# Cross-attention in fp32: one bias sum moved from VectorE to ScalarE and accumulating transfers, and two small reorderings of VectorE's queue

## The chip, the cores and the metric

The kernel runs on one core of one Trainium2 chip. The metric is the device time of one execution in microseconds (us). It is compared as the median of several runs.

## The reference

Two cross-attention layers, one after the other, on 8 batches of 100 queries (width 1024) and 1444 context rows (width 512), all in fp32:

```python
def _L0_xattn_ref(query, key, Wq, bq, Wk, bk, Wv, bv, Wo, bo):
    Q = query @ Wq + bq
    K = key @ Wk + bk
    V = key @ Wv + bv
    weights = softmax(Q @ K.T * scale, axis=-1)        # over the context
    return query + (weights @ V) @ Wo + bo

def _L1_xattn_ref(emb, latent, Wq, bq, Wk, bk, Wv, bv, gamma, beta):
    q, k, v = emb @ Wq + bq, latent @ Wk + bk, latent @ Wv + bv
    w = softmax(q @ k.T * scale, axis=1)               # over the queries
    x = w @ v + emb
    return (x - mean(x)) * rsqrt(var(x) + EPS) * gamma + beta
```

## The kernel before

The kernel never forms K or V. It multiplies weights with weights first: `qk0` = Wq Wk^T of layer 0, `vo0` = Wv Wo of layer 0, later `qk1` for layer 1. Queries then meet the raw context (`s` tiles), the softmax weights are transposed, and the weighted context rows (`A`) go through `vo` (layer 0, the projection, tiles `o_...`) or through Wv (layer 1). Bias terms become sums: the bias that bv brings to the output is bv times Wo, a sum over the 1024 rows of Wo, each scaled by one entry of bv.

The large products use a scheme of seven products of halves in place of eight (the left matrix in blocks A11 to A22, the right in B11 to B22). It needs sums of blocks, S1 to S4 on the left and T1 to T4 on the right, which VectorE makes. Several partial results share banks of PSUM (the matmul accumulators): X, Z, Y and W are such banks. `put` copies a finished bank to SBUF, by ScalarE; `add` adds one to what is already there, by VectorE. A product that accumulates further into a bank has to wait until the `put` or `add` before it has read that bank. An inner call of the same scheme (`inner_product`) splits one of the seven once more; its banks are named `vo_w_x`, `vo_w_z`, `o_w_x` and so on.

TensorE's order is written out by hand (`manual_schedule`). VectorE's calls go through a helper on line 96, so most of its rows have that line; where `vector.in_order` is true they stay in the written order. Each engine works through its own queue in order, so an instruction that waits holds all that stands behind it.

The first place of the change is `weight_products` for `vo0`. The matrices come in eight `unit` tiles (called `vo` in the trace), each with one row block of Wv^T and one of Wo; rows 0 to 3 are blocks 11 and 12 of both sides, rows 4 to 7 blocks 21 and 22. TensorE runs X (A11 B11), Z (A12 B21), Y (S1 T1), then X again with S2 T2. VectorE makes S1 and T1, then T3 (in place of B12), S3 (in place of A21), T2 (in place of B11), later S2 (in place of S1) and T4 (in place of B21). The tiles that hold S1 and then S2 are `vo_s`.

The bias sum of `vo0` is started by `accumulate(1)`, line 465, which calls `transferred_sum` (line 543). Its first half scales rows 0 to 3 of Wo on ScalarE into four tiles (`scaled_sum`, line 569) and adds the tiles pairwise by accumulating transfers issued by GpSimd (`transfer_added`, line 566). Its second half, `second_half`, scales and adds rows 4 to 7 on VectorE in one tile (`prob` in the trace) and adds that by one more transfer. `accs[scaled[0][0]][1]()` calls this second half, on line 500. The finished sum is transposed on VectorE much later (line 585, at 125.35 us).

The second place is `project0` for layer 0, lines 1076 to 1090. There two products in halves run side by side: the outer one uses the banks X_ and Y, an inner one, the generator `W`, yields after each of its seven products. `next(W)` runs the first of them.

Of the kernel before, what the change touches and what calls it, by code (L numbers as in the profile page):

```python
# [27 lines left out]
ALU = mybir.AluOpType  # L28
# [6 lines left out]
EC, LC = E // P, L // P  # L35
# [20 lines left out]
def two_layer_cross_attention(ctx: ExitStack, tc: tile.TileContext, a: dict, out: bass.AP):  # L56
# [11 lines left out]
    def bank(name):  # L68
        return psum.tile([P, 512], F32, tag="ps", name=name)
# [4 lines left out]
    def unit(name):  # L74
        return stream.tile([P, E + L], F32, tag="unit", name=name)
# [4 lines left out]
    def row(name):  # L80
        return work.tile([P, E], F32, tag="row", name=name, bufs=3)

    def weight_rows(name):
        return work.tile([P, MC * T + QD * (-(-T // QD)) - T], F32, tag="wT", name=name, bufs=3)

    def wide_sums(name):
        return work.tile([P, LC, GT], F32, tag="gT", name=name, bufs=3).rearrange("p c t -> p (c t)")
# [13 lines left out]
    vector = Vector()  # L101
# [38 lines left out]
    def run(*parts):  # L140

        parts = list(parts)
        while parts:
            parts = [g for g in parts if next(g, parts) is not parts]
# [8 lines left out]
    def half_product(banks, lhs, rhs, fresh, nb, width):  # L153

        run(half_steps(banks, lhs, rhs, fresh, nb, width))
# [24 lines left out]
    def combine(to, x, y, op, engine=vector):  # L180
        for t, p, q in zip(to, x, y):
            engine.tensor_tensor(t, p, q, op)

    def chunks(t, n):

        return [t[:, i, :] for i in range(n)]
# [68 lines left out]
    def inner_product(name, lhs, rhs, nb, width, t, put, add, right=None, left=None, ahead=False, spare=bank2):  # L255
# [13 lines left out]
        def room(x, t):  # L269
            t = t.rearrange("p (i n) -> p i n", i=m)  # L270
            return [t] if len(x) == 1 else [t[:, i, :] for i in range(m)]
# [5 lines left out]

        S2, S3, S4, T2, T3, T4 = A11, A21, A12, B11, B12, B21
        if ahead:

            S2, S4 = (room(lhs, t[:, o : o + lw]) for o in (lw + rw, 2 * lw + rw))
            if not right:
# [4 lines left out]
        if left:  # L287
            S1, S2, S3, S4 = left

        def second():  # L290
            combine(T2, B22, T1, ALU.subtract)
            combine(S2, S1, A11, ALU.subtract)

        def fourth():
            combine(T4, B21, T2, ALU.subtract)
            combine(S4, A12, S2, ALU.subtract)

# [8 lines left out]
        def product(ps, left, right, fresh):  # L306
            half_product([ps], left, right, fresh, h, w)

        def steps():
# [15 lines left out]
            yield  # L325
            product(X, S2, T2, False)
            put(0, 1, X)
# [19 lines left out]
    def weight_products(name, left, right, l_width, r_width, scaled, between=None):  # L347
# [33 lines left out]
        accs = {}  # L381
# [42 lines left out]
        def pair(n):  # L424
            return [(bank2 if n == "w" else bank)(f"{name}_{n}{j}") for j in range(2)]
# [4 lines left out]
        def block(r, c, j):  # L430

            n = r * nb + j * per
            return dst[:, n : n + per, c * rh : (c + 1) * rh]

        def put(r, c, banks):
            for j in range(2):
                nc.scalar.copy(block(r, c, j), banks[j].rearrange("p (n w) -> p n w", n=per))  # L437

        def add(r, c, banks):
            for j in range(2):  # L440
                to = block(r, c, j)
                vector.tensor_tensor(to, to, banks[j].rearrange("p (n w) -> p n w", n=per), ALU.add)
# [21 lines left out]
        if name == "vo0":  # L464
            accumulate(1)
        put(0, 0, X)
        vector.in_order = name == "vo0"
        combine(T1, B12, B11, ALU.subtract)
        if name == "qk0":
# [3 lines left out]
            Z = pair("z")  # L473
# [6 lines left out]
            W = pair("w")  # L480
# [3 lines left out]
        else:  # L484
            combine(S1, A21, A22, ALU.add)
            Z = pair("z")
# [9 lines left out]
        if name != "qk0":  # L496
            T2, T4 = B11, B21
            combine(T2, B22, T1, ALU.subtract)
            if name == "vo0":
                accs[scaled[0][0]][1]()  # L500
            add(0, 0, Z)
        combine(S1, S1, A11, ALU.subtract)
        S2 = S1
        if name != "vo0":
            combine(A21, A11, A21, ALU.subtract)
        if name != "qk0":
# [7 lines left out]
        t = wide_sums(f"{name}_t")  # L514
# [28 lines left out]
    def transferred_sum(name, srcs, of):  # L543

        n = EC if of == "qk1" else EC // 2
        tiles = [row(f"{name}_{n}") for n in range(2)] + [weight_rows(f"{name}_2")[:, :E]]
        tiles += [t[:, :E] for t in prob]  # L550
        if n == EC:
            tiles += [weight_rows(f"{name}_{n}")[:, :E] for n in range(6, 8)]
        scaled_sum(tiles[:n], srcs[:n])

        def second_half():
            t = tiles[n]
            for i, (src, by) in enumerate(srcs[n:]):
                if i == 0:
                    vector.tensor_scalar(t, src, by, None, ALU.mult)
                else:  # L560
                    vector.scalar_tensor_tensor(t, src, by, t, ALU.mult, ALU.add)
            transfer_added(tiles[0], t)

        return tiles[0], second_half

    def transfer_added(to, t):
        nc.gpsimd.dma_start(out=to, in_=t, accum_op=ALU.add)

    def scaled_sum(tiles, srcs):

        for t, (src, by) in zip(tiles, srcs):
            tc.keep_in_program_order(nc.scalar.activation(t, src, AF.Copy, scale=by))
        k = 1
        while k < len(tiles):
            for i in range(0, len(tiles) - k, 2 * k):
                transfer_added(tiles[i], tiles[i + k])
            k *= 2
# [231 lines left out]
    def first_block_sums():  # L809
# [3 lines left out]
    vo0 = weight_products(  # L813
        "vo0", "L0_xattn_WvT", "L0_xattn_Wo", L, E, (("L0_xattn_bv", 1),), first_block_sums
    )
# [197 lines left out]
    def project0(AS, A0):  # L1013

        B11, B21, B12, B22 = ([A0[g][:, 2 * k + i, :] for i in range(2)] for g in range(2) for k in range(2))
        t12, t4 = (work.tile([P, LC, GT], F32, tag="gT", name=f"o0_t{n}", bufs=3) for n in (12, 4))
        T1, T2, T3, T4 = chunks(t12, 2), [t12[:, 2 + i, :] for i in range(2)], B12, chunks(t4, 2)  # L1020
        h = GT // 2
        room, right = unit("o0_t"), [[t4[:, 2 + n // 2, n % 2 * h : n % 2 * h + h]] for n in range(4)]

        def pair(n, bank=bank):
            return [bank(f"o0_{n}{j}") for j in range(2)]

        def product(banks, lhs, rhs, fresh):
            half_product(banks, lhs, rhs, fresh, 2, GT)

        def add(j, r, g, banks):  # L1030
            e = 4 * j + 2 * r
            add_to_queries([e, e + 1], g * GT, GT, banks)

        def inner(n, j, R, G, lhs, rhs, t, right=None):
            def add(r, c, ps):
                add_to_queries([4 * j + 2 * R + r], G * GT + c * h, h, [ps])

            return inner_product(f"o0_{n}{j}", lhs, rhs, 2, GT, t, add, add, right, ahead=True)

        (A, S), (A_, S_) = AS  # L1040
        X = pair("x")

        def first():
            yield from half_steps(X, A[0], B11, True, 2, GT)
            add(0, 0, 0, X)
            Z = pair("z")
            yield from half_steps(Z, A[1], B21, True, 2, GT)
            add(0, 0, 0, Z)

        yield first()  # L1050
        vector.in_order = True
        yield inner("z", 1, 0, 0, A_[1], B21, room[:, :512], right)
        combine(T1, B12, B11, ALU.subtract)
        X_ = pair("x")
        product(X_, A_[0], B11, True)
        combine(T2, B22, T1, ALU.subtract)
        add(1, 0, 0, X_)
        Y = pair("y")
        product(Y, S[0], T1, True)
        combine(T4, B21, T2, ALU.subtract)  # L1060
        combine(T3, B22, T3, ALU.subtract)
        add(0, 1, 1, Y)
        product(X, S[1], T2, False)
        add(0, 0, 1, X)
        W = pair("w", bank2)
        product(W, A[3], T4, True)
        add(0, 1, 0, W)
        W = inner("w", 1, 1, 0, A_[3], T4, room[:, 512:])
        product(X, S[2], T3, False)
        add(0, 1, 1, X)  # L1070
        add(0, 1, 0, X)
        product(Y, S[3], B22, False)
        add(0, 0, 1, Y)
        yield

        Y = pair("y")
        product(Y, S_[0], T1, True)
        Q = inner("q", 1, 0, 1, S_[3], B22, room[:, :512], right)
        add(1, 1, 1, Y)
        product(X_, S_[1], T2, False)  # L1080

        next(W)
        add(1, 0, 1, X_)
        run(W)
        add(1, 0, 1, Y)
        product(X_, S_[2], T3, False)
        run(islice(Q, 4))
        add(1, 1, 1, X_)
        add(1, 1, 0, X_)
        run(Q)  # L1090
        vector.in_order = False
# [241 lines left out]
    for bs in SETS:  # L1333
        t = wide(f"A1T_{bs[0]}").rearrange("p c t -> p (c t)")[:, : LC * len(bs) * T]
        t = t.rearrange("p (c t) -> p c t", c=LC)
# [39 lines left out]
```

## Time and profile before

| | us |
|---|---|
| runs shown | 634.80, 634.42, 633.78 |
| median | 634.42 |
| profiled execution, its own time | 634.84 |
| its span in the trace | 632.9 |
| TensorE busy | 621.5 |
| VectorE busy | 487.1 |
| ScalarE busy | 163.9 |

The span is the time from the first to the last recorded instruction. PE is TensorE's matmul side and PEld its loading of weights; DVE is VectorE, ACT ScalarE, POOL GpSimd and SP SyncE, and a "q" behind a name is that engine's issuing of transfers. In rows of groups the name before "<-" is what is written and the names behind it are what is read. In a timeline a row begins with start and duration, and the brackets give the idle time just before it and what ended it. An fp32 matmul appears as two records.

### The profile page before, as it was taken

The numbers are of one execution on the slowest core, as the hardware profiler recorded it, in microseconds if no ns is written. First come the engines' busy times: TensorE is split into PE (matmuls) and PEld (weight loads), VectorE is DVE, ScalarE is ACT, GpSimd is POOL, SyncE is SP. The second block draws the span as 40 slices with busy tenths as digits, with TensorE's granted clock in tenths as the row PEclk, the third lists the DMA queues.
The fourth block names the chain that finished last, engine by engine and source line by source line (L and its number), as shares of the span: only waits on it lengthen the run. The fifth ranks groups of instructions, "written<-read, shape, count | busy, mean of one in ns | idle before, by whom it ended". The sixth has DMA issues, their size and how long they took to land.

```text
span 632.9 us, 10570 instructions
## 1 busy us (share of the span) xinstructions
PE 621.5 (98%) x4142; PEld 534.2 (84%) x4142; DVE 487.1 (77%) x995; ACT 163.9 (26%) x380; POOL 102.2 (16%) x133
## 2 busy tenths in 40 slices
PE   9999999999999999999999999999999999999994
PEld 8886467688985999999989666756999999999992
DVE  2987979996885797666758687968777659898886
ACT  1322012324304234423230001113433240325301
POOL 2110101112230000000000001008111220544054
PEclk9999999999999999999999999999999999999998
DMA  8969848335999788988942308255888990599002
GB/s 272 293 136 348 274 140 272 68 81 111 203 315 382 283 311 299 327 307 306 312 155 88 101 0 325 96 194 192 295 305 307 316 324 2 201 330 332 27 22 84
DMA packets 52521, 138.27 MB, mean 218 GB/s; under 512 B 4403, under 2 KB 8755, under 8 KB 52471
## 3 DMA queue, kind: packets, MB, share of 16 engines
q1 hardware_dynamic: 46792, 120.85, 55.1%
q0 software_dynamic: 5280, 16.26, 11.7%
q8 instruction: 33, 0.54, 0.3%
q10 hardware_dynamic: 398, 0.47, 0.2%
q14 instruction: 18, 0.14, 0.1%
HBM read 123.36 MB, written 3.28 MB: 200 GB/s over the span
## 4 chain that ended last, share of the span: by engine, by line
PE 90%; DMA 3%; DVE 3%; issue 1%; POOL 1%; ACT 0%; POOLq 0%; DVEq 0%; SPq 0%
PE s L923 25%; PE A L894 25%; PE qk_x L163 6%; PE o_x L163 5%; PE g_x L163 4%; DMA vo<-in_L_xattn_Wo 3%; PE o_y L163 3%; PE g_y L163 3%; PE vo_x L163 2%; PE qk_y L163 2%; PE qk_z L163 2%; DVE vo L96 1%; PE o_z L163 1%; PE o_w L163 1%; PE qk_w L163 1%
## 5 line engine op out<-in xcount | busy, mean ns | idle before, releaser
L894 PE MATMUL A<-w,c 120*128 120x100 f32 (+1 forms) x1536 | 249.6, 265 | 0.0
L894 PEld LDWEIGHTS A<-w,c 120*128 120x128 f32 (+1 forms) x1536 | 218.0, 190 | 2.8
L96 DVE STREAM_TRANSPOSE w<-prob 32x384 f32<-32x384 f32 (+1 forms) x256 | 143.7, 561 | 27.6 <-ACT prob L962 9.7
L923 PE MATMUL s<-cT,g1T 128*100 128x131 f32 (+2 forms) x592 | 122.8, 296 | 0.0
L923 PE MATMUL s<-cT,g0T 128*100 128x131 f32 (+2 forms) x592 | 122.7, 296 | 0.0
L923 PEld LDWEIGHTS s<-cT,g1T 128*100 128x100 f32 x592 | 78.4, 167 | 8.6 <-issue 0.3
L923 PEld LDWEIGHTS s<-cT,g0T 128*100 128x100 f32 x592 | 78.2, 167 | 8.4 <-PE c L593 0.4
L935 ACT ACTIVATE prob<-s,c 100x393 f32<-100x393 f32 (+2 forms) x64 | 34.5, 560 | 112.7 <-PE s L923 99.5
L1111 ACT ACTIVATE w<-w,negmax 120x100 f32<-120x100 f32 (+1 forms) x96 | 34.8, 364 | 82.7 <-DVE negmax L96 82.7
L955 DVE TENSOR_REDUCE maxima<-prob 100x1 f32<-100x394 f32 (+3 forms) x32 | 16.5, 528 | 23.4 <-ACT prob L935 23.1
L1321 POOL DMA_DIRECT2D wv<-in_L_xattn_Wv x1 | 0.8, 772 | 191.2 <-PE o_x L163 191.2
L163 PE MATMUL qk_x<-qk 128*128 128x256 f32 x128 | 29.7, 380 | 0.0
L1130 POOL TENSOR_TENSOR part<-w 120x500 f32<-120x500 f32 x8 | 10.9, 1368 | 112.9 <-DVE rstd L1205 28.6
L163 PEld LDWEIGHTS qk_x<-qk 128*128 128x128 f32 x128 | 23.3, 190 | 3.0 <-ACT qk L437 0.2
L669 ACT ACTIVATE g1T<-g_x,k 128x400 f32<-128x400 f32 x4 | 2.4, 594 | 69.2 <-PE g_x L163 69.0
L1111 ACT ACTIVATION_READ_ACCUMULATOR w<-w,negmax 120x1 f32 (+1 forms) x96 | 17.9, 187 | 0.0
L1210 POOL TENSOR_TENSOR z<-z,vectors 100x1024 f32<-100x1024 f32 x7 | 16.5, 2356 | 8.2 <-ACT z L1209 8.2
L96 DVE TENSOR_TENSOR xT<-xT,o_x 128x400 f32<-128x400 f32 (+1 forms) x32 | 15.8, 539 | 2.2 <-PE o_x L163 2.0
L1188 PE MATMUL z<-ident,xT 128*100 128x128 f32 x64 | 16.3, 273 | 0.0
L1209 ACT ACTIVATE z<-z,rstd 100x1024 f32<-100x1024 f32 x7 | 8.0, 1149 | 31.9 <-POOL rstd L1206 31.9
L1192 DVE SCALAR_TENSOR_TENSOR z<-vectors,r,z 100x512 f32<-100x512 f32 x16 | 11.8, 740 | 4.8 <-PE z L1188 4.8
L163 PE MATMUL vo_x<-vo 128*128 128x512 f32 x32 | 15.3, 595 | 0.0
(415 smaller groups left out, 987.8 us busy)
## 6 DMA issues: line engine op xcount, KB each, us to landing
cT<-in_ctxT SPq DMA_DIRECT2D x64, 722.0 KB, 6.3
c<-in_ctx SPq DMA_DIRECT2D x48, 768.0 KB, 8.3
c<-in_ctx SPq DMA_DIRECT2D x16, 512.0 KB, 5.9
vo<-in_L_xattn_Wo SPq DMA_DIRECT2D x8, 512.0 KB, 10.1
qk<-in_L_xattn_WqT SPq DMA_DIRECT2D x8, 512.0 KB
qk<-in_L_xattn_WqT SPq DMA_DIRECT2D x15, 256.0 KB, 5.8
c<-in_ctx SPq DMA_DIRECT2D x16, 224.0 KB, 5.9
xT<-in_xT SPq DMA_DIRECT2D x2, 1600.0 KB
```

Of the source, the lines that this page charges most:

```text
L96: ins = getattr(nc.vector, op)(*args, **kw)
L163: nc.tensor.matmul(banks[n // per][:, n % per * width : (n % per + 1) * width], lhs[i][:, n * P : (n + 1) * P], rhs[i], start=(fresh and i ...
L894: nc.tensor.matmul(ps[:, k * T : (k + 1) * T], c[m // CQ][:r, m % CQ, k * P : (k + 1) * P], w[:r, m, :], start=(m == 0 and k == 0), stop=( ...
L923: nc.tensor.matmul(banks[n // per][:T, cuts[n] - o : cuts[n + 1] - o], q[:, k, t0 : t0 + T], cT[k][:, cuts[n] : cuts[n + 1]], start=(k == ...
L935: nc.scalar.activation(p[:, part], ps[:T, : part.stop - part.start], AF.Identity, bias=key_bias[layer][:T, b : b + 1], scale=SCALE,)
L955: nc.vector.tensor_reduce(maxima[:, n : n + 1], p[:, part], AX.X, ALU.max)
L1111: nc.scalar.activation(w[:r, m0 + m, :], w[:r, m0 + m, :], AF.Exp, bias=negmax[:r, m : m + 1], accum_out=total[:r, m : m + 1])
L1130: add(part, w[:MR, 0:5, :], w[:MR, 5:10, :], ALU.add)
L1188: nc.tensor.transpose(ps[:T, e * P : (e + 1) * P], xT[:, 4 * j + e, b * T : (b + 1) * T], ident)
L1192: nc.vector.scalar_tensor_tensor(z[:, half], bv1[j][:T], s["r"], ps[:T, :], ALU.mult, ALU.add)
L1209: nc.scalar.activation(z, z, AF.Copy, scale=rstd)
L1210: nc.gpsimd.tensor_tensor(z, z, beta[:T], ALU.add)
```

## The change

In `vo0` the second half of the bias sum is made like the first: four scaled tiles by ScalarE, added pairwise by transfers. It is called right after the copies of the first X product, and no longer from VectorE's sequence of sums. Two more tiles of the pool "wT" are taken for it. VectorE's four operations for the sum are gone, GpSimd issues three transfers more. Still in `vo0`, the two additions of Z move behind the four operations that make S2. In `project0` the two additions of X_ move behind four additions of the inner product, where they stood behind one.

```diff
@@ weight_products
         put(0, 0, X)
+        if name == "vo0":
+            accs[scaled[0][0]][1]()
         vector.in_order = name == "vo0"
...
             combine(T2, B22, T1, ALU.subtract)
-            if name == "vo0":
-                accs[scaled[0][0]][1]()
-            add(0, 0, Z)
+            if name != "vo0":
+                add(0, 0, Z)
         combine(S1, S1, A11, ALU.subtract)
         S2 = S1
+        if name == "vo0":
+            add(0, 0, Z)
...
@@ transferred_sum
-        if n == EC:
+        if of != "qk0":
             tiles += [weight_rows(f"{name}_{n}")[:, :E] for n in range(6, 8)]
         scaled_sum(tiles[:n], srcs[:n])
 
         def second_half():
             t = tiles[n]
-            for i, (src, by) in enumerate(srcs[n:]):
-                if i == 0:
-                    vector.tensor_scalar(t, src, by, None, ALU.mult)
-                else:
-                    vector.scalar_tensor_tensor(t, src, by, t, ALU.mult, ALU.add)
+            if of != "qk0":
+                scaled_sum(tiles[n:], srcs[n:])
+            else:
+                for i, (src, by) in enumerate(srcs[n:]):
+                    if i == 0:
+                        vector.tensor_scalar(t, src, by, None, ALU.mult)
+                    else:
+                        vector.scalar_tensor_tensor(t, src, by, t, ALU.mult, ALU.add)
             transfer_added(tiles[0], t)
@@ project0
-        next(W)
+        run(islice(W, 4))
         add(1, 0, 1, X_)
         run(W)
```

## The prediction

> **What bounds the kernel now.** I read the page's busy table first, then the waits of TensorE, then the order of time on TensorE and VectorE around each wait. The table says that TensorE works nearly all the time:
>
> ```profile
> PE 621.5 (98%) x4142; PEld 534.2 (84%) x4142; DVE 487.1 (77%) x995; ACT 163.9 (26%) x380; POOL 102.2 (16%) x133
> ```
>
> So only TensorE's idle time can be saved, unless matmuls go, and the change touches none. The view of TensorE's waits lists every one of them:
>
> ```profile
> PE warm L108 <- DVE ones L105: 1.1, 1, 1.1
> PE vo_x L163 <- DVE vo_s L96: 1.0, 1, 1.0
> PE o_w_y L163 <- DVE xT L96: 0.6, 1, 0.6
> PE g_z_x L163 <- DVE g_t L96: 0.4, 1, 0.4
> ```
>
> The second and third stand at the two places that the change edits. The first is the timeline of VectorE and TensorE near 65 to 75 us (start, duration, what, and in brackets the idle time before it):
>
> ```profile
> 65.41 2.49 DVE L96 TENSOR_TENSOR vo<-vo,vo_s 128x512 f32<-128x512 f32 x4
> 67.82 0.74 DVE L96 TENSOR_SCALAR prob<-vo,L_xattn_bv 128x1024 f32<-128x1024 f32 x1
> 68.60 3.92 DVE L96 SCALAR_TENSOR_TENSOR prob<-vo,L_xattn_bv,prob 128x1024 f32<-128x1024 f32 x3
> 72.44 1.28 DVE L96 TENSOR_TENSOR vo<-vo,vo_z 128x512 f32<-128x512 f32 x2
> 73.63 1.43 DVE L96 TENSOR_TENSOR vo_s<-vo_s,vo 128x256 f32<-128x256 f32 x4
> 74.97 2.49 DVE L96 TENSOR_TENSOR vo<-vo,vo 128x512 f32<-128x512 f32 x4
> ```
>
> ```profile
> 59.27 7.03 PE L163 MATMUL vo_z<-vo 128*128 128x512 f32 x16
> 66.13 7.03 PE L163 MATMUL vo_y<-vo_s 128*128 128x512 f32 x16
> 74.20 7.10 PE L163 MATMUL vo_x<-vo,vo_s 128*128 128x512 f32 x16 [1.04 <-DVE vo_s L96]
> 81.14 1.03 PE L163 MATMUL vo_w_x<-vo 128*128 128x256 f32 x4
> ```
>
> VectorE works through T2, the bias sum (four operations) and the additions of Z before S2; S2's first piece ends about 74.05, and TensorE starts X at 74.20. The second place is in the projection of layer 0:
>
> ```profile
> 374.31 0.50 PE L163 MATMUL o_w_w<-o_t,vo 128*128 128x200 f32 x2
> 375.37 0.60 PE L163 MATMUL o_w_y<-o_t,o_t 128*128 128x200 f32 x2 [0.56 <-DVE xT L96]
> 375.81 0.50 PE L163 MATMUL o_w_x<-o_t,vo 128*128 128x200 f32 x2
> 376.15 2.85 PE L163 MATMUL o_x<-A0T,vo 128*128 128x400 f32 x8
> ```
>
> ```profile
> 373.45 0.36 DVE L96 TENSOR_TENSOR xT<-xT,o_w_x 128x200 f32<-128x200 f32 x1 [0.41 <-PE o_w_x L163]
> 373.73 1.05 DVE L96 TENSOR_TENSOR xT<-xT,o_x 128x400 f32<-128x400 f32 x2
> 374.69 0.35 DVE L96 TENSOR_TENSOR xT<-xT,o_w_z 128x200 f32<-128x200 f32 x1
> 374.96 0.35 DVE L96 TENSOR_TENSOR xT<-xT,o_w_y 128x200 f32<-128x200 f32 x1
> ```
>
> The second Y product overwrites a bank that the addition at 374.96 must have read (done 375.31). That addition stands behind the two of X_.
>
> **What the Trainium skill says.** "Perfetto Trace Analysis", section "Tensor Engine Instruction (MATMUL, LD_WEIGHTS)": the end of a matmul is an estimate, its start is recorded. The trace agrees: the 16 of Z end at 66.30, after Y's start at 66.13. I therefore count from start to start. "ScalarE: Activation LUTs", section "What ACT_TABLE_LOAD costs": an ACTIVATE with one pointer operand takes about 280 ns + 0.833 ns per element, an estimate of 1.13 us for 1024; the trace has 1.149, which I use. "DMA: Bandwidth & Descriptors", sections "SWDGE vs HWDGE vs iDMA" and "Issuing engines are not separate DMA queues": only GpSimd issues accumulating transfers, and all queues share the same 16 engines. All such transfers in the trace stand on GpSimd's queue. "SBUF — State Buffer", section "Who interferes with whom": a tensor_tensor with both inputs in SBUF contends with GpSimd's reads, not its writes; no row here shows such contention, so I bound it below.
>
> **Part 1, the bias sum and S2.** Before, rows 4 to 7 of Wo were summed on VectorE: 0.74 + 3.92 = 4.7 us. Now ScalarE scales each row: 4 x 1.149 = 4.6 us, right after the two copies of X (they start 58.61 and 59.47, end 60.06). It needs the rows of Wo; VectorE's own wait for the last row ended at 63.46, so the rows are there by then. ScalarE ends near 64.7 (60.06 + 4.6; from the last row's landing, 63.46 + 1.15 = 64.6). Behind them on ScalarE stand the copies of Y, which before started at 72.34 after 12.29 us of idle time: cost nothing, with over 7 us of cover. The sum moves to three more transfers on GpSimd (prob1 += prob2, vo_6 += vo_7, prob1 += vo_6), ahead of the last one. Transfers of this size landed 5.6 to 9.0 us after issue, median 8.3. GpSimd issues at 63.37 (as before), about 64.3 and 65.2, then near 74 and 83; the sum is whole near 92 instead of 82. Its reader is the VectorE transpose at 125.35: 33 us of cover. GpSimd's next work stands at 108.01. GpSimd's three issues take 0.86 us each; if each held VectorE up wholly, that is 2.6 us before T2 is done, at 70.5, still ahead of X.
>
> S2 writes over S1 in place, so it cannot all move to 67.9: its four pieces wait for Y's four row blocks. Y's 16 matmuls take 66.13 - 59.27 = 6.86 us; its quarters are over about 67.85, 69.56, 71.28 and 72.99. ScalarE's copy of Y's last bank began 73.20, so a release takes about 0.2. S2's pieces (0.42 each) then end near 68.5, 70.2, 71.9 and 73.6. VectorE sits between them, and Z's additions, T4 and the four W sums are queued behind the fourth. Z's additions run 73.5 to 74.8, T4 74.8 to 77.2, the W sums to 79.4; before, the last two ended 77.4 and 79.6. So nothing gets later, though the 4.7 us that VectorE saves become idle time. TensorE needs S2's first piece at 72.99 and its fourth 5.1 us later, and T4 at 79.85: all there. The copies of X that X's accumulation needs were over at 60.06.
>
> Gain: without the stall X starts at 72.99 instead of 74.20, and the next group at 66.13 + 2 x 6.86 = 79.85 instead of 81.14: **1.29 us** (the wait view's 1.04 is the lower reading).
>
> What is late next: VectorE idles 2.16 us before 81.77 and 0.96 before 84.00, each time released by TensorE. With TensorE 1.29 earlier and VectorE 0.2 ahead, about 1.1 of the first is left and the 0.96 stays. VectorE is nearly full from there to 110, but its work starts from these releases and moves with them. So the stall of 0.4 at 108.31 stays, and the loads of the next weights (issued from 84.78 as matrices come free) move too.
>
> **Part 2, the projection.** The additions of w_z, w_y and the second w_x go ahead of X_'s two. From TensorE's starts plus the 0.2 release, VectorE runs them at 373.79, 374.13 and 374.51, and X_'s at 374.79 and 375.27. The addition of w_y ends 374.48, so the second Y product starts 0.34 after w_w, at 374.65; w_x follows at 374.99 (its bank free at 374.92), o_x at 375.33. o_x overwrites X_'s first bank, read until 375.31, with 0.06 to pass on (375.31 to 375.37 above): 375.37. Its second bank is free at 375.85, needed at 376.04. Gain 376.15 - 375.37 = **0.78 us** (lower reading 0.56). VectorE's next wait, 1.43 us for o_q_x, shows it isn't behind; nothing is late next.
>
> Sum: 1.29 + 0.78 = 2.07. The profiled execution's own time is 634.84 with a span of 632.9: span to 630.8, own time to 632.8. The median of the runs shown is 634.42, 0.42 lower; minus 2.07 it is **632.4**.
>
> **The rivals.** *Only part of a stall goes.* If S2's pieces were all held to Y's end (73.2), X would start near 73.7: part 1 brings 0.5, the sum 1.3, 633.1. If X_'s additions keep o_x waiting, part 2 brings nothing: 633.1 too. If both, 633.9. Against: S2 is four operations on separate row blocks; for: margins of 0.04 to 0.1 us in part 2. *The gain is given back* at 108.31, if VectorE does not move with TensorE: the stall grows by 1.29, leaving 0.78, 633.6. Against: the idle 0.96 at 84.00. *Slower: the three transfers hold up xT.* They fall in the stretch where the DMA engines are full:
>
> ```profile
> 60.00:70.00 10.00, 10.00 (x25) 4.38 (x24) 8.70 (x16) 0.05 (x1) 0.85 (x1) 1.00 1.07 333
> 70.00:80.00 10.00, 8.96 (x22) 3.86 (x21) 9.58 (x20) 1.17 (x2) 0.86 (x1) 1.00 0.67 201
> 80.00:90.00 10.00, 10.00 (x36) 6.35 (x35) 7.26 (x23) 2.66 (x6) 0.00 (x0) 1.00 0.32 93
> ```
>
> (the last two columns are the DMA share and GB/s). xT was issued at 53.17, behind the last row of Wo; SyncE issues nothing between 64.37 and 84.78. The share falls to 0.67 in 70 to 80, so I take xT as landed near 77; its first use is the product at 100.2, now 98.9. It decides once xT is over 22 us later. At worst all three, at 9.0 us, go ahead of it: 77 + 27 = 104, TensorE waits 5.1, net +3.0: 637.4. Sharing makes it far less likely.
>
> **Numbers.** Both stalls go 0.70; partly 0.13; given back 0.07; slower 0.10, with what I don't see. A measurement of this kernel tells some 0.2% (1.27 us) from no change: the partial cases lie around that edge. Faster 0.74, same 0.15, slower 0.11. Range 631.5 (the third stall of 0.4 goes too, and the runs' own spread of half a us) to 634.4 (partial cases and given back; it leaves out the slower one).
>
> **What would show it.** TensorE's waits without vo_x and o_w_y; X 6.86 us after Y's start; S2's pieces spread from 68 to 73.6 with VectorE idle between them; ScalarE's four near 60 to 65; o_x 1.45 us after w_x's second start (before 376.15 - 373.92 = 2.23). Wrong if a wait of TensorE for xT, vo or vo_w takes their place, or the wait at g_z_x grows.

## The result, and the profile after

| | before | after |
|---|---|---|
| median of 20 runs each, us | 635.32 | 633.95 |
| mean of 20 runs each, us | 635.13 | 633.97 |
| profiled execution, own time, us | 634.84 | 633.66 |
| its span, us | 632.9 | 631.8 |

The ratio of after to before is 0.9982, with an interval of [0.9975, 0.9988]: faster, by 0.8 to 1.6 us. The forecast was a gain of 2.07; the gain is a little over half of that. The median of 633.95 lies in the stated range of 631.5 to 634.4, which says little: the range reaches up to the time of before that the forecast started from (634.42), and the runs of before timed beside after are slower than those (635.32).

The page's busy table of after:

```profile
PE 621.5 (98%) x4142; PEld 534.6 (85%) x4142; DVE 482.7 (76%) x991; ACT 168.0 (27%) x384; POOL 104.8 (17%) x136
```

VectorE has four instructions fewer and 4.4 us less to do, ScalarE four more and 4.1 us, GpSimd three more. TensorE's busy time is the same. All of TensorE's waits in after:

```profile
PE warm L108 <- DVE ones L105: 1.1, 1, 1.1
PE g_z_x L163 <- DVE g_t L96: 0.4, 1, 0.4
```

Both waits that the forecast named are gone, no wait for `xT` or `vo` took their place, and the wait at `g_z_x` did not grow. TensorE around X in after (start, duration, what):

```profile
59.61 7.03 PE L163 MATMUL vo_z<-vo 128*128 128x512 f32 x16
66.48 7.03 PE L163 MATMUL vo_y<-vo_s 128*128 128x512 f32 x16
73.34 7.03 PE L163 MATMUL vo_x<-vo,vo_s 128*128 128x512 f32 x16
80.21 1.03 PE L163 MATMUL vo_w_x<-vo 128*128 128x256 f32 x4
```

X starts 6.86 us after Y. From Z's start to `vo_w_x` it is 20.60 us, 21.87 before: 1.27 less, where 1.29 was forecast. VectorE in the same stretch of after:

```profile
64.73 2.49 DVE L96 TENSOR_TENSOR vo<-vo,vo_s 128x512 f32<-128x512 f32 x4
68.39 0.42 DVE L96 TENSOR_TENSOR vo_s<-vo_s,vo 128x256 f32<-128x256 f32 x1 [1.18 <-PE vo_y L163]
70.11 0.42 DVE L96 TENSOR_TENSOR vo_s<-vo_s,vo 128x256 f32<-128x256 f32 x1 [1.29 <-PE vo_y L163]
71.83 0.42 DVE L96 TENSOR_TENSOR vo_s<-vo_s,vo 128x256 f32<-128x256 f32 x1 [1.29 <-PE vo_y L163]
73.54 0.42 DVE L96 TENSOR_TENSOR vo_s<-vo_s,vo 128x256 f32<-128x256 f32 x1 [1.29 <-PE vo_y L163]
73.89 1.28 DVE L96 TENSOR_TENSOR vo<-vo,vo_z 128x512 f32<-128x512 f32 x2
75.08 2.49 DVE L96 TENSOR_TENSOR vo<-vo,vo 128x512 f32<-128x512 f32 x4
```

S2's four pieces are spread out behind Y's row blocks, and the time that VectorE saves has become idle time, as the brackets show. TensorE itself is now what VectorE waits for. The bias sum on ScalarE and GpSimd in after:

```profile
60.29 2.19 ACT L578 ACTIVATE prob<-vo,L_xattn_bv 128x1024 f32<-128x1024 f32 x2
62.38 2.17 ACT L578 ACTIVATE vo_L_xattn_bv<-vo,L_xattn_bv 128x1024 f32<-128x1024 f32 x2
```

```profile
63.40 0.85 POOL L573 DMA_DIRECT2D vo_L_xattn_bv<-vo_L_xattn_bv  x1 [9.04 <-issue]
63.94 1.19 POOL L573 DMA_DIRECT2D prob<-prob  x1
64.85 1.17 POOL L573 DMA_DIRECT2D vo_L_xattn_bv<-vo_L_xattn_bv  x1
77.95 0.86 POOL L573 DMA_DIRECT2D prob<-vo_L_xattn_bv  x1 [11.93 <-DMA vo_L_xattn_bv<-vo_L_xattn_bv]
84.71 0.86 POOL L573 DMA_DIRECT2D vo_L_xattn_bv<-prob  x1 [5.90 <-DVE vo L96]
```

The third transfer landed 12.6 us after its issue (5.6 to 9.0 for the transfers of this sum in before), and the last was issued at 84.71, where the forecast had near 83. The reader now starts at 124.42: the cover was never near its end.

The projection in after, TensorE and then VectorE:

```profile
373.38 0.50 PE L163 MATMUL o_w_w<-o_t,vo 128*128 128x200 f32 x2
373.72 0.57 PE L163 MATMUL o_w_y<-o_t,o_t 128*128 128x200 f32 x2
374.12 0.50 PE L163 MATMUL o_w_x<-o_t,vo 128*128 128x200 f32 x2
374.48 2.95 PE L163 MATMUL o_x<-A0T,vo 128*128 128x400 f32 x8
377.27 0.50 PE L163 MATMUL o_q_x<-A0T,o_s 128*128 128x200 f32 x2
```

```profile
373.27 0.36 DVE L96 TENSOR_TENSOR xT<-xT,o_w_y 128x200 f32<-128x200 f32 x1
373.58 0.36 DVE L96 TENSOR_TENSOR xT<-xT,o_w_x 128x200 f32<-128x200 f32 x1
373.86 1.04 DVE L96 TENSOR_TENSOR xT<-xT,o_x 128x400 f32<-128x400 f32 x2
```

From `o_w_w` to `o_q_x` it is 3.89 us, 4.53 before (374.31 to 378.84): 0.64 less, where 0.78 was forecast.

So TensorE's two stages are 1.27 + 0.64 = 1.91 us shorter, and yet the two profiled executions differ by 1.18 in their own times, and the means by 1.15. In the two traces 0.34 of the rest lies ahead of Z, which starts at 59.61 in place of 59.27, and 0.47 behind the last product. The experiments ask whether these two are chance.

### The profile page after: what moved, and what is told of

It reads as the page before. It is cut to its first block, busy times and chain, and to the rows that moved or that the text cites. A ratio compares the mean times of both kernels' runs of the same rounds, so it can differ in the third digit from the quotient of the medians.

```text
span 631.8 us, 10578 instructions
## 1 busy us (share of the span) xinstructions
PE 621.5 (98%) x4142; PEld 534.6 (85%) x4142; DVE 482.7 (76%) x991; ACT 168.0 (27%) x384; POOL 104.8 (17%) x136
## 4 chain that ended last, share of the span: by engine, by line
PE 95%; DVE 2%; issue 1%; POOL 1%; POOLq 0%; ACT 0%; DVEq 0%
PE s L929 25%; PE A L900 25%; PE qk_x L163 7%; PE o_x L163 5%; PE g_x L163 4%; PE vo_x L163 3%; PE o_y L163 3%; PE g_y L163 3%; PE qk_z L163 2%; PE qk_y L163 2%; PE o_z L163 1%; PE o_w L163 1%; PE qk_w L163 1%; PE vo_y L163 1%; PE vo_z L163 1%; PE z L1194 1%
## 5 line engine op out<-in xcount | busy, mean ns | idle before, releaser
L675 ACT ACTIVATE g1T<-g_x,k 128x400 f32<-128x400 f32 x4 | 2.4, 594 | 68.5 <-PE g_x L163 68.4
```

## The experiments

Ratios are to the kernel before on the same chip. Spans are those of the profiled execution.

**Each part alone, and both kernels again.** `c_part1` has the bias sum and S2 changed, with the projection as before. `c_part2` has only:

```diff
-        next(W)
+        run(islice(W, 4))
```

`c_before` and `c_after` are the two kernels unchanged.

> The kernel before, unchanged, as the yardstick for chance. Theory A (the traces' own stretches tell the change: part 1 brings 1.28 us, part 2 brings 0.64, and the 0.35 us that the changed kernel lost before the first full-speed product and the 0.46 that it lost after the last product are chance): ratio 1.0000 within 0.001; the first product of vo (vo_z) starts anywhere within 59.2 to 59.7 us, and the time from the last product to the end of the span varies by some tenths. Theory B (the change itself costs at the start or at the end): the same ratio, vo_z at 59.27 and the same tail as in the first profile of the kernel before, within 0.1 us.

> Only the bias sum and S2 are changed; the projection stays as it was. Theory A: TensorE's wait at vo_x is gone, the one at o_w_y (0.6) is back; from vo_z to vo_w_x 20.60 us (before 21.87), from o_w_x to o_q_x 5.93; 1.28 us less, ratio 0.9980. Theory B with the cost in part 1 (its longer queues of GpSimd and ScalarE or its transfers): ratio 0.9992, some 0.5 us less, with the start or the tail longer by 0.4 each as in the changed kernel.

> Only the two additions of the projection are moved. Theory A: TensorE's wait at o_w_y is gone, that at vo_x (1.0) stays; from o_w_x to o_q_x 5.29 us (before 5.93); 0.64 us less, ratio 0.9990. Theory B with the cost in part 2: ratio 1.000, the gain given back after the projection.

> The changed kernel once more. Theory A: both stretches as in its first profile (20.60 and 5.29), 1.92 us less from vo_z to the last product; start and tail differ from those of its first profile by tenths; ratio 0.9970 to 0.9982. Theory B: vo_z again near 59.6 and the tail again some 0.5 us longer than before's; ratio 0.9982.

| | median, us | ratio, interval | span | vo_z starts | X starts | X behind Y | end behind the last product |
|---|---|---|---|---|---|---|---|
| c_before | 635.23 | 0.9999 [0.9990, 1.0008] | 633.3 | 59.41 | 74.57 | 8.29 | 8.40 |
| c_part1 | 634.68 | 0.9989 [0.9982, 0.9995] | 632.2 | 59.30 | 73.03 | 6.87 | 8.91 |
| c_part2 | 634.71 | 0.9993 [0.9981, 1.0004] | 633.0 | 60.80 | 74.92 | 7.25 | 8.37 |
| c_after | 634.13 | 0.9988 [0.9981, 0.9994] | 633.0 | 60.75 | 74.48 | 6.86 | 8.88 |

Part 1 alone gains some 0.7 us, nearer to theory B's 0.5 than to theory A's 1.28; part 2's interval includes no gain, and `c_after` gained less than either theory had. Each part takes away its own wait in its profile and no other. Two things were new. First, TensorE comes to this stage at different times in different executions of the same kernel (59.41 and 59.27 in two profiles of before, 60.75 and 59.61 in two of after), and in `c_part2`, where it comes late, the wait for X is short. TensorE in `c_part2`, and then in `c_after`:

```profile
67.67 7.03 PE L163 MATMUL vo_y<-vo_s 128*128 128x512 f32 x16
74.92 3.24 PE L163 MATMUL vo_x<-vo,vo_s 128*128 128x512 f32 x7 [0.22 <-DVE vo_s L96]
```

```profile
67.62 7.03 PE L163 MATMUL vo_y<-vo_s 128*128 128x512 f32 x16
74.48 4.03 PE L163 MATMUL vo_x<-vo,vo_s 128*128 128x512 f32 x9
```

With nearly the same late Y, part 1 is worth 0.4 here, not 1.2. Second, with part 1 in the kernel the time from the last product's end to the end of the span is longer: 8.84 to 8.91 in every profile of after, `c_after` and `c_part1`, 8.37 to 8.42 in every profile of before and in `c_part2`. So the start moves by chance, whichever the kernel (theory A, and by more than its 59.2 to 59.7), and the end goes with part 1 (theory B).

**A later start of TensorE.** Four more warming products ahead of the first real one, in before (`w_before`) and in after (`w_after`):

```diff
-    for _ in range(8):
+    for _ in range(12):
         nc.tensor.matmul(warm[:, :P], ones, ones, start=True, stop=True)
```

> The kernel before with 12 warming matmuls in place of 8, which makes TensorE's first product start later, by about 0.86 us at full clock (8 records of 0.108). Theory C (in the kernel before, the stall at vo_x takes up what TensorE loses at its start, because X waits there for VectorE, which waits for the last rows of the matrices; in the changed kernel nothing takes it up): vo_z starts later, the stall at vo_x is shorter by about as much, and the time rises by only 0.2 to 0.5 us (ratio 1.0003 to 1.0008). Theory A (chance alone): the time rises by the whole 0.86, ratio 1.0014, with the stall at its 1.0 to 1.3.

> The changed kernel with 12 warming matmuls in place of 8. Theory C: no stall is there to take the delay up, so the changed kernel gets slower by the whole 0.86 us and its gain over the kernel before falls from about 1.0 to about 0.2: ratio 0.9995 to 1.0001. Theory A: the same 0.86 is lost, but in both kernels, so that this one stays 1 us below the other with 12.

The ratios were 1.0013 [1.0006, 1.0021] and 0.9992 [0.9984, 1.0001]. This missed. Before should have hidden part of the delay in its wait, and it got slower by 0.8 us; the changed kernel's gain did not shrink (0.9992 / 1.0013 = 0.9979). The profile of `w_before` does have a short wait (0.4 us), but VectorE's wait for the last row of Wv^T ended at 62.32, later than in any other profile of before. The traces show why the wait hides nothing. SyncE's issue of that row, in before and then in `w_before` with its Z:

```profile
51.95 0.36 SPq L376 DMA_DIRECT2D vo<-in_L_xattn_WvT  x1
```

```profile
53.55 0.36 SPq L376 DMA_DIRECT2D vo<-in_L_xattn_WvT  x1
60.86 7.03 PE L163 MATMUL vo_z<-vo 128*128 128x512 f32 x16
```

The issue stands 7.31 or 7.32 us ahead of Z's start in all 14 profiles: the loads go out as TensorE moves on, and a late TensorE makes them late by as much. The pair therefore moved both sides of the wait and could not tell how long it usually is.

**The wait at vo_x in other executions of before.** Three single profiled runs of the kernel before, unchanged:

> The kernel before, for one more sample of its stall at vo_x. Theory C': X starts there when VectorE has finished, which follows the landing of the matrices and only in part TensorE's own start, so that the stall from start to start is anywhere from 0.4 us (TensorE late, vo_z near 60.8) to 1.4 (TensorE early, vo_z near 59.3). Theory A: it is 1.2 to 1.4 whenever vo_z starts.

> As the first look: Theory C' has a short stall beside a late vo_z and a long one beside an early vo_z; Theory A has 1.2 to 1.4 in any case.

> As the first look: Theory C' has a short stall beside a late vo_z and a long one beside an early vo_z; Theory A has 1.2 to 1.4 in any case. Over all samples Theory C' has a mean stall well under the 1.2 of the first profile.

They gave 634.46, 635.42 and 635.63 us. X in each of the three, `look1` first (TensorE):

```profile
73.73 7.11 PE L163 MATMUL vo_x<-vo,vo_s 128*128 128x512 f32 x16
```

```profile
74.53 7.11 PE L163 MATMUL vo_x<-vo,vo_s 128*128 128x512 f32 x16 [1.11 <-DVE vo_s L96]
```

```profile
74.99 7.10 PE L163 MATMUL vo_x<-vo,vo_s 128*128 128x512 f32 x16 [1.82 <-DVE vo_s L96]
```

The wait that the forecast took as 1.04 to 1.29 is nothing, 1.1 and 1.8 in three executions of one kernel, and the times follow it. That contradicts theory A. Theory C' holds in part only: the spread is wider than its 0.4 to 1.4, the shortest wait does not stand beside the latest Z (59.82 in `look1`, 60.80 in `c_part2`), and the mean of the six profiles of this stage without part 1, counted from start to start, is 1.07, not well under 1.2. What sets the wait is on VectorE, in `look1` and then in `look3`:

```profile
60.09 0.43 DVE L96 TENSOR_TENSOR vo_s<-vo,vo 128x256 f32<-128x256 f32 x1 [1.67 <-DMA vo<-in_L_xattn_WvT]
60.44 1.89 DVE L96 TENSOR_TENSOR vo<-vo,vo 128x512 f32<-128x512 f32 x3
62.99 0.69 DVE L96 TENSOR_TENSOR vo<-vo,vo 128x512 f32<-128x512 f32 x1 [0.67 <-DMA vo<-in_L_xattn_Wo]
```

```profile
62.10 0.43 DVE L96 TENSOR_TENSOR vo_s<-vo,vo 128x256 f32<-128x256 f32 x1 [3.95 <-DMA vo<-in_L_xattn_WvT]
62.45 2.49 DVE L96 TENSOR_TENSOR vo<-vo,vo 128x512 f32<-128x512 f32 x4
```

VectorE waits for the last rows of the matrices and then runs a chain of fixed length up to S2. Where the row of Wo is what it waits for last, X starts 10.74 us behind that wait: 62.99 to 73.73 in `look1`, 63.46 to 74.20 in before, 64.18 to 74.92 in `c_part2`. Where the row of Wv^T is last it is 12.88 (61.65 to 74.53 in `look2`), 12.89 in `look3` (62.10 to 74.99) and 12.87 in `w_before`; in `c_before`, with a little more waiting in between, 13.10. So in before a landing decides when X starts, and TensorE's wait is what is left between the two. The issue of the load follows TensorE; what varies by itself is the time from there on: VectorE's wait for the last row of Wv^T ended 7.6 to 10.1 us after its issue in the six profiles. With part 1 the chain is 4.7 us shorter, and VectorE has idle time ahead of S2's first piece in all six profiles taken with 8 warming products (0.29 to 1.18 us): in none of them does a landing reach X, which follows Z by 13.73 or 13.74 us in each.

The mean over the six profiles without part 1 and with 8 warming products (before, c_before, c_part2, the three looks) puts X at 74.49; over the six with part 1 (after, c_after, c_part1, and t_pool, g_stall and best below) at 73.53. That is 0.96 us, against 1.21 in the forecast (74.20 to 72.99). Six profiles tell such a mean to about 0.3 only, and Z happened to start 0.11 later in the second six; counted from Z's start, the difference is 1.07. So the profiles alone do not tell the mean from the forecast.

The spans of all runs do. From X's start to the end of the span it is 558.71 to 558.78 us in the five profiles of before, and 558.48 and 558.53 in the two of after: what lies behind X takes the same time in each. If that holds for the runs without a profile too, a run's span tells when its X started. The mean start is then 74.44 in the 113 runs of before taken beside the experiments and 73.71 in the 41 runs of after and `c_after` (20 and 21). The difference is **0.73**, to about 0.2.

**The longer end.** `t_pool` is after, with three clearings moved so that GpSimd has 133 instructions again, as before:

```diff
     for t in prob:
-        nc.gpsimd.memset(t[:, S:], 0.0)
+        nc.vector.memset(t[:, S:], 0.0)
```

> The changed kernel with the three clearings of the ends of the prob tiles on VectorE in place of GpSimd, so that GpSimd has three instructions less, as many as the change gave it more. Theory D (the 0.3 us that both kernels with part 1 lose between the landing of the last output and the end of the span come from where GpSimd's last instructions lie in its stream): the time from the last product to the end falls from 8.84 to 8.91 to about 8.55, and the time by 0.3 us, ratio 0.9980. If the tail comes from the transfers or the work: 8.84 to 8.91 as before, ratio 0.9985.

The ratio was 0.9974 [0.9964, 0.9985], the median 633.83. The end behind the last product is 8.21 us, shorter than the 8.55 that theory D had, and shorter than in before. After was not timed on this chip, and its intervals on the others overlap with this one, so it is the trace that shows the effect and not the time. The last arithmetic and the last store's issue, in the timelines of all engines of after, of `t_pool` and of before (VectorE's last row, then ScalarE's queue; of before also VectorE's row at L1205):

```profile
625.98 1.41 DVE L1221 SCALAR_TENSOR_TENSOR z<-z,rstd,vectors 100x512 f32<-100x512 f32 x2 [0.44 <-POOL rstd L1212]
...
627.42 0.56 ACTq L1222 DMA_DIRECT2D out<-z  x1
```

```profile
626.88 1.42 DVE L1221 SCALAR_TENSOR_TENSOR z<-z,rstd,vectors 100x512 f32<-100x512 f32 x2 [0.44 <-POOL rstd L1212]
...
628.33 0.57 ACTq L1222 DMA_DIRECT2D out<-z  x1
```

```profile
626.10 0.15 DVE L1205 TENSOR_SCALAR rstd<-mv 100x1 f32<-100x1 f32 x1 [0.46 <-DVE mv L1203]
...
627.89 1.41 DVE L1215 SCALAR_TENSOR_TENSOR z<-z,rstd,vectors 100x512 f32<-100x512 f32 x2 [0.44 <-POOL rstd L1206]
...
629.33 0.57 ACTq L1216 DMA_DIRECT2D out<-z  x1
```

Measured from the last product's end (624.54 in before, 622.99 in after, 623.89 in `t_pool`), the issue comes at 4.79, 4.43 and 4.44 us: with part 1 it is even 0.36 earlier, since VectorE's wait of 0.46 at L1205 is gone. But SyncE saw the store landed at 7.48, 7.64 and 7.31, so it took 2.68, 3.20 and 2.87 us. And the last two steps of GpSimd, which release the last steps of the other engines, are 0.08 apart in before and in `t_pool`, and 0.38 apart in after. (These steps are semaphore records of the traces, which the views leave out.) The balance for after is -0.36 + 0.52 + 0.30 = +0.46, what its span shows (8.84 against 8.37). In `t_pool` the 0.30 is gone, and 0.33 of the 0.52. The 0.38 is there in all five profiles with 136 instructions on GpSimd, and in none of the nine with 133. So the end goes with GpSimd's count, some 550 us behind the place where the three added instructions stand. The edit of `t_pool` also brings VectorE's count from 991 to 994 (995 in before), and no run separates the two; the 0.30 lies on GpSimd itself, but for the store's landing either count could stand. Why a count matters there is not settled. The Trainium skill, "Runtime: NRT & Kernel Launch", section "Instruction fetch mechanics", says that each engine fetches its instructions in blocks of 256; a block boundary that has moved into the end would fit, but the packets of the instruction queue near the end do not line up with the steps, and I do not call it shown.

Of the 0.47 that the span grows, 0.13 comes back outside it: a run's own time is 1.83 to 1.86 us above its span in the kernels with 136 instructions on GpSimd, 1.98 in the runs of `c_before`. That leaves 0.34.

**The wait that stayed.** `g_stall` is after, with four of Z's inner products put ahead of S1's sums in layer 0's first stage of queries:

```diff
-                combine(S1, A21, A22, ALU.add)
                 combine(T1, B12, B11, ALU.subtract)
+                run(islice(Z, 4))
+                combine(S1, A21, A22, ALU.add)
                 run(Z)
```

> The changed kernel with the next stall attacked in the same way: in the first queries product, VectorE's sum S1 (1.22 us) moves behind the first four steps of the inner product, so that the inner product's second sums come 1.2 us earlier. If the wait at g_z_x (0.4, from start to start 0.57) is VectorE's order alone, TensorE's list of waits keeps only the warming one and the time falls by 0.4 to 0.5 us more: ratio 0.9976 to 0.9981. If S1 comes too late for the outer Y product, a wait at g_y takes its place, ratio 0.9985.

The ratio was 0.9979 [0.9969, 0.9990], as expected, but too near to after's to show a gain by itself. The trace shows it: only the wait for the first warming product is left on TensorE, and from X's start to the last product's end it is 549.26 us, 549.64 in after. So 0.38 is gained and not given back. `best` joins both edits:

> The changed kernel with both further edits: S1 of the first queries product behind four inner steps, and the three clearings on VectorE. If the two gains add up (0.38 on TensorE at g_z_x, 0.5 at the end), the time falls by some 0.9 below the changed kernel: ratio to the kernel before 0.9966 to 0.9976, and TensorE waits for nothing but the first ones. If the place of GpSimd's last instructions is what counts and moves again, the tail is back at 8.8 to 8.9 us and the ratio near 0.998.

It ran at 632.64 us in five runs, 0.9963 [0.9950, 0.9977], a little beyond the 0.9966 to 0.9976 expected if the two gains add up. It is faster than before, and probably than after, whose interval begins at 0.9975. The end behind the last product is 8.26 us. TensorE's waits and its `g_z_x` in `best`:

```profile
PE warm L108 <- DVE ones L105: 1.1, 1, 1.1
```

```profile
105.84 0.84 PE L163 MATMUL g_z_y<-g_t,g_t 128*128 128x200 f32 x4
106.67 0.94 PE L163 MATMUL g_z_x<-g_t,g_t 128*128 128x200 f32 x4
```

The product that waited 0.41 us in after now starts 0.83 us behind its forerunner, which was 1.25 in after.

## Why the prediction was wrong, point by point

**Where the waits go: right.** Both left TensorE, by the mechanism that the prediction gave. S2's pieces were to end near 68.5, 70.2, 71.9 and 73.6; less the 0.35 us by which this execution's TensorE ran later, they end at 68.46, 70.18, 71.90 and 73.61. ScalarE's four scalings take 4.26 us, forecast 4.6. The idle times ahead of VectorE's next two waits are 1.12 and 0.96, forecast about 1.1 and 0.96. The wait at `g_z_x` stays at 0.4.

**The size of part 1: wrong.** The step that failed is "without the stall X starts at 72.99 instead of 74.20". It fits the execution that it was read from (1.27 between the two traces), and it took that execution's wait as the kernel's. X's start in before hangs on a landing whose time from issue moves by up to 2.5 us from one execution to the next. By the spans of all runs X comes 0.73 earlier in the mean, and between X and `vo_w_x` another 0.07 is saved (6.94 to 6.87): 0.80 in place of 1.29. The prediction had a sign of it and did not use it: it names VectorE's wait for the last row, which ended at 63.46, and still counts the start of S2 as given.

**The size of part 2: a little too large.** 0.64 in place of 0.78. VectorE does what was forecast, to 0.01: the addition of the second `o_w_x` 0.20 behind `o_w_w`, X_'s two 0.28 later. The term that was mis-sized is the bank that passes from VectorE to TensorE. "w_x follows at 374.99", 0.34 behind w_y, was 0.40, `o_x` followed by 0.36 and not by 0.38, and `o_x`'s second record follows its first by 0.44, not 0.34: 0.06 - 0.02 + 0.10. The first record of `o_x` is 0.60 long in after and 0.50 in before and in `c_part1`, where X_'s additions are over earlier; that fits a product which is recorded as started while it still waits for its bank, though no run tests this by itself. The prediction took 0.06 "to pass on" from one start alone. Its own rows show the rest: `o_w_y`, which waits in before, is followed after 0.44 (375.37 to 375.81), not 0.34.

**The three transfers: no cost where they stand, but a longer end.** The rival in which they hold up `xT` did not happen: `xT` is first used at 99.30 without a wait. DMA stayed full 10 us longer, as these two rows of after's table by stretch show (share and GB/s last; 0.67 and 0.32 before):

```profile
70.00:80.00 10.00, 10.00 (x25) 4.47 (x24) 7.02 (x17) 1.62 (x3) 0.86 (x1) 1.00 1.05 282
80.00:90.00 10.00, 10.00 (x36) 6.65 (x35) 8.16 (x25) 2.21 (x6) 0.86 (x1) 1.00 0.76 176
```

The step that failed is the one that ends at "GpSimd's next work stands at 108.01": the prediction followed the three instructions to their neighbours and not to the program's end, where the last store's landing and GpSimd's last steps set the span. That term stood at nothing and is 0.34.

**The sum.** 0.73 + 0.07 + 0.64 - 0.34 = 1.10, in place of 2.07. The runs measured 1.15 in the means of 20 each (interval 0.8 to 1.6), and 0.92 beside `c_after` (0.4 to 1.2). The sum agrees with both. Since the 0.73 is worked out from the spans of these runs, that says only that no further loss is left over; with the 0.96 of the profiles the sum is 1.33.

## What to carry to other kernels

A wait in one profile is a sample. Before it is priced, ask what ends it: if a landing does, its time from issue varies, and the wait can be zero in the next execution. A few more profiles of the same kernel show the spread, and where nothing behind the wait moves, the spans of all runs tell its mean. And when instructions are added to an engine that closes the program, compare the end of the span behind the last product as well: nothing there shows as a wait of TensorE.

## What the runs showed of the hardware

TensorE's clock at the start is low for a time that differs from run to run. In the 14 traces the record of the granted clock goes to the full rate between 4.1 and 7.3 us. Where that is behind the first real product (at 4.6 us), the real products ahead of it follow each other at 0.427 us, and those behind it at 0.216. The Trainium skill, "TensorE: Matmul & The Clock Gate", section "What's actually happening", says that the number of slow first products varies from run to run; here it moves Z's start from 59.27 (full rate from 4.13) to 60.80 us (from 7.28) in kernels with the same work ahead of it. Since the loads go out as TensorE moves on, this goes into the time of both kernels.
